# Conv sequence, frequency gate: product and sum on GpSimd, ScalarE in emission order, inverse roots by logarithm and exponential

## The chip, the core and the metric

The kernel runs on one core of one Trainium2 chip. Such a core has five engines with queues of their own: TensorE (PE, matrix products; its weight loads are shown apart as PEld), VectorE (DVE), ScalarE (ACT), GpSimd (POOL) and SyncE (SP, which here issues most DMAs). The metric is the device time of one execution in microseconds; lower is better. Times of several runs are given as a median with the lowest and the highest.

## The reference, cut to what matters

Four layers follow each other on `x` of shape 4 x 192 x 64 x 64 (image, channel, row, column). Layer 0 is a deformable convolution with an attention over channels and an MLP; layer 1 a non-local block over all 4096 pixels; layer 2 a window attention, a frequency gate and a gated MLP; layer 3 a small convolution whose weights come from the image's mean. The change lies in the frequency gate of layer 2 and what stands around it:

```python
def _hft(x, w, b):
    a = 3.0 * x
    for s in (2, 4, 8):
        pool = x.reshape(B, C, h // s, s, ww // s, s).mean(axis=(3, 5))
        a = a - jnp.repeat(jnp.repeat(pool, s, axis=2), s, axis=3)
    return jax.nn.sigmoid(_dwconv3(a, w, b)) * x

out = (o_img / s_img[:, :, None]).reshape(B, C, H, W)
out = _hft(_conv1x1(out, proj_w, proj_b), hft_w, hft_b)
x1 = x + out
z = jax.nn.gelu(_conv1x1(_ln_c(x1, n2g, n2b), fc1_w, fc1_b), approximate=False)
```

So the attention's output is projected (a 1x1 convolution), three pooled versions of it are taken off three times itself, a depthwise 3x3 convolution and a sigmoid make a gate of that, the gate multiplies the projection, and the product is added to the image. A layer norm over the channels and the MLP follow. A layer norm needs `1 / sqrt(variance + 1e-5)` at each pixel.

## The kernel before

The four images go through the layers one after the other. While image `b` is in its last part, `rest` (projection with the gate, MLP, layer 3), parts of image `b + 1` are woven in: `rest` pulls steps of two generators, `main` (image `b`) and `other` (`mlp0`, the layer-0 MLP of image `b + 1`), and takes a step of `other` whenever the numbers yielded by `main` add up to 1. The last image has nothing beside it (`alone`), and there a part of the depthwise taps is done on PE as products with diagonal matrices (`HFT_PE`, L1368) instead of DVE.

`project` works on six units. Units 0 to 3 are sixteen rows each of channels 0 to 127; units 4 and 5 hold the remaining 64 channels, two halves of the image on the two halves of the partitions. Every unit is 128 partitions x 1024 numbers. For each unit there are two steps:

- `first(u)`: two projected halves on PE (L1475, L1478), copied out of PSUM by ACT with the bias into `pr` (L1482); the pooling sums by DVE (L1490, L1493) and their way back (L1499); three times `pr` by ACT (L1505) and minus the means by DVE (L1513) into `hft`, or into `others` in the image's tile `x` for units 4 and 5; then `share(u)` copies rows at the units' edges, by GpSimd (L1454, L1455) or, for units 4 and 5, by DMAs that SP issues (L1466).
- `second(u)`: the depthwise convolution `depthwise_steps` by DVE into `acc` (named `ha` in the profile; L1373 the first tap, L1377 the others), the sigmoid by ACT (L1523), the product with `pr` (L1525) and the sum into `x` (L1526), both by DVE.

They are emitted in this order: first 0, first 1, second 0, first 2, second 1, first 4, first 5, second 4, first 3, second 2, second 5, then `ahead` (the layer norm of the first pair of rows for the MLP, `pair_norm_steps`, tiles `d_l2n` and `r_l2n`), second 3. `pr` has four buffers, `acc` two.

In which order the instructions of an engine stand in its queue is decided when the program is built: a scheduler chooses by its own estimates of costs, unless code stands inside `tc.manual_schedule()`, where an engine keeps the order of emission. The window attention before `project` and the MLP after it are inside such blocks, for all engines; `project` is not. Whatever the order, each queue is worked off in order.

ScalarE evaluates functions from a table set, and a change of the set is an instruction of its own (ACT_TABLE_LOAD in the profile). The list `in_order` tells whether a part is emitted in order. If it isn't empty, `table(name)` emits a load whenever the set changes, and `inverse_root_steps` takes logarithm and exponential on ACT (L353, L354, one table set for both). If it is empty, `table` does nothing, the loads are put in by the compiler, and the inverse root is a square root on ACT (L362) and a reciprocal on DVE (L364):

```python
if in_order:
    inverse_root(r, pv)
    yield VARIANCE
else:
    nc.scalar.activation(r, pv, AF.Sqrt, bias=eps)
    yield VARIANCE
    nc.vector.reciprocal(r, r)
```

The layer norms that `mlp0` computes while `project` runs (`norm_steps`, tiles `xa`, `d_l0m`, `r_l0m`; L793, L796) use the same function. Other names of `mlp0` in the profile: `h` (L844, L851) and `gl` (L858) are the widened activations before and after GELU, `o` the narrowed output or the attention's, which L874, L775 and L786 add into `xa`; L894 stores `xa`.

Of the kernel before, what the change touches and what calls it, by code (L numbers as in the profile page):

```python
# [12 lines left out]
AF = mybir.ActivationFunctionType  # L13
ALU = mybir.AluOpType
# [16 lines left out]
UN = UR * W  # L31
HEADS = 6
NEG = -1.0e30
LN_EXP, GELU = "natural_log_exp_and_others", "gelu"

# [40 lines left out]
GATE_PE, GATE_PE_LAST, HFT_PE = (0, 1), (0, 1, 2, 3, 4), (0, 1, 2, 3, 4)  # L78
# [3 lines left out]
def conv_seq_kernel(ctx: ExitStack, tc: tile.TileContext, a, out: bass.AP):  # L82
    nc = tc.nc

    def pool_of(**kw):

        return tc.tile_pool(**({} if kw.get("space") == DRAM else {"reuse_waits": "tile"}), **kw)
# [251 lines left out]
    in_order = []  # L339

    def table(name):

        if in_order and in_order[0] != name:
            in_order[0] = name
            if name == GELU:
                nc.scalar.preload_act_table(AF.Gelu)
            else:
                nc.scalar.preload_act_table_set(name)

    def inverse_root(r, pv):  # L350

        table(LN_EXP)
        nc.scalar.activation(r, pv, AF.Ln, bias=eps)  # L353
        nc.scalar.activation(r, r, AF.Exp, scale=-0.5)  # L354
# [64 lines left out]
    def links(steps, upto=None):  # L419

        while True:
            try:
                link = next(steps)
                if upto is not None and link == upto:
                    return None
            except StopIteration as end:
                return end.value
# [311 lines left out]
    def mlp0(b, m2, pool, sb, ps):  # L739
# [95 lines left out]
        for i in range(NCH):  # L835
# [3 lines left out]
            def widen(ms):  # L839

                banks = [ps.tile([128, 2, HN], F32, tag="h", name=f"h_{b}_{i}_{ms[0]}_{q}") for q in range(2)]
                for j, m in enumerate(ms):
                    for q in range(2):
                        nc.tensor.matmul(  # L844
                            banks[q][:, j, :], lhsT=fc1[:, 0, bass.ts(m, 128)], rhs=hn[:, bass.ts(q, HN)], start=j == 0,
                            stop=False, skip_group_check=True,
                        )
                for j, m in enumerate(ms):
                    for q in range(2):
                        rows = slice(Q * q, Q * q + Q)  # L850
                        nc.tensor.matmul(  # L851
                            banks[q][:, j, :], lhsT=fc1[rows, 1, bass.ts(m, 128)], rhs=hn[rows, CN:], start=False, stop=True,
                            skip_group_check=True,
                        )
                for j, m in enumerate(ms):
                    for q in range(2):
                        table(GELU)
                        nc.scalar.activation(  # L858
                            gl[:, m, bass.ts(q, HN)], banks[q][:, j, :], AF.Gelu, bias=fc1_bias[:, m : m + 1]
                        )  # L860
# [189 lines left out]
    def windows(b, oi, load_image):  # L1050
# [3 lines left out]
        with ExitStack() as s:  # L1054
# [227 lines left out]
            with tc.manual_schedule():  # L1282
# [3 lines left out]
                norm(0, SQUARE)  # L1286
                in_order.append(None)
                table(LN_EXP)
                norm(0, VARIANCE)
                keep_warm(warm, 2)  # L1290
# [60 lines left out]
    def depthwise_steps(strip, w, diag, taps, acc, ps, name):  # L1351


        parts, blocks, rows = strip.shape[0], strip.shape[1], strip.shape[2] - 2
        acc = acc.rearrange("p (b r c) -> p b r c", b=blocks, c=W)

        def src(tap, b=slice(None), r=0, n=rows):
            return strip[:, b, tap // 3 + r : tap // 3 + r + n, tap % 3 : tap % 3 + W]

        others = [tap for tap in range(9) if tap not in taps]  # L1360
        first = others.pop(0)
        if taps:
            n = CN // W
            for b in range(blocks):
                for r in range(0, rows, n):
                    p = ps.tile([128, CN], F32, tag="t", name=f"{name}_{b}_{r}")[:parts]
                    for j, tap in enumerate(taps):
                        nc.tensor.matmul(p, lhsT=diag[:, j, :], rhs=src(tap, b, r, n), start=j == 0, stop=j == len(taps) - 1)  # L1368
                    to, p = acc[:, b, r : r + n], p.rearrange("p (r c) -> p r c", c=W)
                    nc.vector.scalar_tensor_tensor(to, src(first, b, r, n), w[:, first : first + 1], p, ALU.mult, ALU.add)  # L1370
        else:
            for b in range(blocks):
                nc.vector.tensor_scalar_mul(acc[:, b], src(first, b), w[:, first : first + 1])  # L1373
        yield first
        for tap in others:
            for b in range(blocks):
                nc.vector.scalar_tensor_tensor(acc[:, b], src(tap, b), w[:, tap : tap + 1], acc[:, b], ALU.mult, ALU.add)  # L1377
            yield tap
# [44 lines left out]
    def project(b, x, others, oi, ps, taps, ahead):  # L1423
# [3 lines left out]
        with ExitStack() as s:  # L1427
# [5 lines left out]
            tiles, prs = {}, {}  # L1433
            row = slice(1, W + 1)

            def get(u):

                if u not in tiles:
                    t = tiles[u] = held[:, u % 3] if u < 4 else others[:, u - 4]
                    nc.gpsimd.memset(t[:, :, :, 0:1], 0.0)  # L1440
                    nc.gpsimd.memset(t[:, :, :, W + 1 : W + 2], 0.0)

                    for v, parts, k, r in (
                        (0, slice(0, M), 0, 0), (3, slice(0, M), 0, UR + 1), (4, half(0), 0, 0), (5, half(1), 1, 9),
                    ):
                        if u == v:
                            nc.gpsimd.memset(t[parts, k, r, row], 0.0)
                return tiles[u]
# [67 lines left out]
            def second(u):  # L1516
                k = u // 4
                acc = sb.tile([M, UN], F32, tag="acc", name=f"ha_{b}_{u}")
                diag = hft_diag[:, k] if taps else None
                for tap in depthwise_steps(get(u), VW["l2_hftw"][:, k], diag, taps, acc, ps, f"ht_{b}_{u}"):  # L1520
                    if tap % 3 == 2:
                        yield
                nc.scalar.activation(acc, acc, AF.Sigmoid, bias=VW["l2_hftb"][:, k])  # L1523
                cols = bass.ts(u, UN)
                nc.vector.tensor_tensor(acc, acc, prs.pop(u), ALU.mult)  # L1525
                nc.vector.tensor_tensor(x[:, cols], x[:, cols], acc, ALU.add)  # L1526


            for of, u in (
                (first, 0), (first, 1), (second, 0), (first, 2), (second, 1), (first, 4), (first, 5), (second, 4),  # L1530
                (first, 3), (second, 2), (second, 5), (None, 0), (second, 3),
            ):
                if of is first:
                    first(u)
                    yield 0.33
                elif of is second:
                    for _ in second(u):
                        yield 0.5
                else:
                    ahead()  # L1540
# [306 lines left out]
    def rest(b, x, others, oi, sums, m2):  # L1847


        with ExitStack() as s:  # L1850
            alone = m2 is None
            sb = s.enter_context(pool_of(name="norms", bufs=1))
            ps = s.enter_context(pool_of(name="restps", bufs=2, space=PSUM))
            wide = s.enter_context(pool_of(name="restps2", bufs=5, space=PSUM))
            psums = Psums({"n": ps, "v": ps, "h": wide}, {"t": "h"})
            other = iter(())
            if not alone:
                other = mlp0(b + 1, m2, s.enter_context(pool_of(name="l0d", bufs=1)), sb, psums)
            credit = 0.0

            def main():
                hn = []

                def ahead():
                    hn.append(links(pair_norm_steps(x, 0, sb, psums, f"l2n2_{b}_0")))

                yield from project(b, x, others, oi.pop(), psums, HFT_PE if alone else (), ahead)
                yield from mlp(b, x, sums, sb, psums, GATE_PE if alone else (), hn)
                yield from layer3(b, x, sums, psums, alone)

            for part in main():
                credit += part
                while credit >= 1.0:
                    next(other, None)
                    credit -= 1.0
            for _ in other:
                pass
# [53 lines left out]
    for b in range(B):  # L1931
# [25 lines left out]
        x = big.tile([M, UNITS * UN + 2 * 2 * 10 * (W + 2)], F32, tag="x", name=f"x_{b}")  # L1957
        others = x[:, UNITS * UN :].rearrange("p (v k r c) -> p v k r c", v=2, k=2, c=W + 2)
# [9 lines left out]
        oi = big.tile([P, 2, HW], F32, tag="x", name=f"oi_{b}")  # L1968
# [79 lines left out]
```

## Time and profile before

| | |
|---|---|
| median of 3 runs | 6800.64 us (6798.39 to 6806.05) |
| the profiled execution | 6757.88 us, span from first to last instruction 6756.1 us |
| busy share of the span | PE 91%, PEld 62%, DVE 69%, ACT 53%, POOL 31% |
| mean granted PE clock | 0.952 |
| chain that ended last, by engine | PE 51%, DVE 17%, ACT 4%, issue 4%, DMA 2% |
| `project` runs, from the first L1475 on | 1866, 3460, 5044 and 6339 us after the start, for 105 to 134 us each |
| sigmoids L1523 | 24 x, median 1149 ns |
| products L1525 | 24 x, median 1218 ns |

A profile is of one execution. Its page gives the busy time of each engine, the chain of work that ended last (followed back from the last instruction, at each step to what released it), and groups of instructions with their number, busy time, mean duration, and the idle time of the engine just before them with what ended it. The same can be asked for a stretch of time. Engines work beside each other: only what lies on the chain of a stretch sets its end.

### The profile page before, as it was taken

Reading aid. Unit: us, or ns where it says so; the run is one execution under the profiler, and the core shown is the slowest. Engines: PE = TensorE matmul, PEld = TensorE weight load, DVE = VectorE, ACT = ScalarE, POOL = GpSimd, SP = SyncE. Lnnn points to the kernel's source line nnn. Section 1 sums busy time; section 2 is a strip of 40 time slices with the busy share of each in tenths; the row PEclk is TensorE's granted clock in tenths of the full one; section 3 lists DMA queues with packets and bytes.
Section 4 is the critical chain, followed back from the end, with each engine's and each line's share of the span. In section 5 each row is a group of like instructions: output and inputs, shape, how many; then the busy total and the mean of one; then the engine's idle time right before and its main releaser. Section 6 shows DMA issues by size and latency. Waiting matters only on the chain.

```text
span 6756.1 us, 115795 instructions
## 1 busy us (share of the span) xinstructions
PE 6155.1 (91%) x45392; PEld 4180.0 (62%) x45392; DVE 4694.1 (69%) x6908; ACT 3599.2 (53%) x6136; POOL 2065.4 (31%) x2276
## 2 busy tenths in 40 slices
PE   7687999999989899999998899999998889999986
PEld 4455578786644458887654457878664457776532
DVE  3664279985677758996576848988567867765656
ACT  3664368774444358885444338877444435544332
POOL 2654057662200027672210007765220000012200
PEclk8788999999989899999999999999999999999998
DMA  6885156661010156663110047665101010010000
GB/s 188 260 280 177 54 177 217 215 196 42 8 43 15 59 181 200 219 211 93 29 31 26 17 132 218 216 208 165 35 24 30 17 54 10 15 28 22 4 7 21
DMA packets 330496, 699.37 MB, mean 104 GB/s; under 512 B 60077, under 2 KB 217181, under 8 KB 329182
## 3 DMA queue, kind: packets, MB, share of 16 engines
q0 software_dynamic: 92736, 455.22, 21.0%
q1 hardware_dynamic: 236382, 235.95, 12.3%
q8 instruction: 358, 5.87, 0.4%
q14 instruction: 188, 1.54, 0.1%
q10 hardware_dynamic: 832, 0.79, 0.0%
HBM read 611.25 MB, written 78.87 MB: 102 GB/s over the span
## 4 chain that ended last, share of the span: by engine, by line
PE 51%; DVE 17%; ACT 4%; issue 4%; DMA 2%; SPq 0%; POOL 0%; another core or an unknown queue 0%; DVEq 0%; ACTq 0%; POOLq 0%
PE y L1031 8%; PE s L963 7%; PE h L634 3%; PE v L1196 2%; PE h L1574 2%; DVE ha L1377 2%; PE qk L1121 2%; PE qk L1122 2%; PE t L1204 1%; DVE gate L1377 1%; PE zm L1586 1%; DVE ga L1377 1%; PE h L1576 1%; PE s L1157 1%; PE rb L1270 1%
## 5 line engine op out<-in xcount | busy, mean ns | idle before, releaser
L616 POOL DMA_INDIRECT ring<-table,idx x1152 | 1634.7, 1419 | 1132.5 <-issue 217.8
L963 PE MATMUL s<-ths,ph 96*128 96x256 f32 x4096 | 991.5, 383 | 8.5 <-ACT xo L626 2.7
L963 PEld LDWEIGHTS s<-ths,ph 96*128 96x128 f32 x4096 | 784.0, 193 | 137.1 <-ACT ths L957 4.7
L622 ACT ACTIVATE row<-ring,pos 128x384 f32<-128x384 f32 x1152 | 672.0, 608 | 204.3 <-DVE xo L627 111.3
L1031 PE MATMUL y<-sc,gx 128*97 128x256 f32 x3008 | 724.7, 383 | 18.4 <-ACT yn L1037 15.1
L623 DVE SCALAR_TENSOR_TENSOR row<-ring,fr,row 128x384 f32<-128x384 f32 x1152 | 674.8, 613 | 91.6 <-ACT row L622 63.1
L1031 PEld LDWEIGHTS y<-sc,gx 128*97 128x97 f32 x3008 | 492.5, 165 | 150.8 <-ACT yn L1037 16.5
L626 ACT ACTIVATE xo<-row,pos 128x192 f32<-128x192 f32 x1152 | 485.8, 448 | 156.9 <-remote 63.8
L627 DVE SCALAR_TENSOR_TENSOR xo<-row,fr,xo 128x192 f32<-128x192 f32 x1152 | 447.1, 412 | 123.3 <-issue 60.6
L1028 DVE TENSOR_TENSOR sc<-sc,mbs 128x1024 f32<-128x1024 f32 x376 | 453.4, 1218 | 46.1 <-ACT mbs L989 26.5
L965 ACT COPY sc<-s 128x1024 f32<-128x1024 f32 x376 | 377.5, 1004 | 177.5 <-PE s L963 141.5
L970 DVE TENSOR_TENSOR top<-top,sc 128x1024 f32<-128x1024 f32 x282 | 344.5, 1222 | 137.4 <-ACT sc L965 115.9
L634 PE MATMUL h<-ti,xo 128*128 128x192 f32 x2304 | 437.1, 328 | 0.0
L1029 ACT ACTIVATE sc<-sc 128x1024 f32<-128x1024 f32 x376 | 393.4, 1053 | 75.6 <-DVE sc L1028 66.5
L634 PEld LDWEIGHTS h<-ti,xo 128*128 128x128 f32 x2304 | 390.9, 190 | 29.0 <-issue 8.6
L1180 DVE TENSOR_REDUCE es<-ex 128x6 f32<-128x384 f32 x264 | 133.3, 546 | 365.0 <-ACT ex L1176 365.0
L634 PE MATMUL h<-kept,xo 128*128 128x192 f32 x960 | 255.9, 402 | 114.1 <-DVE xo L627 61.5
L634 PEld LDWEIGHTS h<-kept,xo 128*128 128x128 f32 x960 | 183.0, 224 | 209.5 <-DVE xo L627 98.6
L1624 POOL COPY gate<-gate 128x192 f32<-128x192 f32 x12 | 4.2, 351 | 1000.4 <-ACT gate L1617 855.0
L1377 DVE SCALAR_TENSOR_TENSOR ga<-gate,v,ga 128x1024 f32<-128x1024 f32 x234 | 300.4, 1284 | 6.7
L1031 PE MATMUL y<-se,gx 128*97 128x256 f32 x1088 | 268.3, 387 | 8.6 <-ACT se L1029 8.1
L858 ACT ACTIVATE gl<-h,bias_fc 128x256 f32<-128x256 f32 x384 | 151.2, 474 | 232.9 <-PE h L851 232.5
(391 smaller groups left out, 11213.0 us busy)
## 6 DMA issues: line engine op xcount, KB each, us to landing
ti<-table SPq DMA_DIRECT2D x768, 48.0 KB
ring<-table,idx POOLq DMA_INDIRECT x1152
xnd<-xn SPq DMA_DIRECT2D x4, 3270.0 KB
xi<-in_x_dram SPq DMA_DIRECT2D x32, 384.0 KB
xk<-xd SPq DMA_DIRECT2D x32, 384.0 KB
xd<-xc SPq DMA_DIRECT2D x64, 192.0 KB
table<-tt SPq DMA_DIRECT2D x32, 384.0 KB
xc<-xd SPq DMA_DIRECT2D x60, 192.0 KB
```

Of the source, the lines that this page charges most:

```text
L616: nc.gpsimd.indirect_dma_start(out=gt.rearrange("p q r c -> p (q r c)"), out_offset=None, in_=corners, in_offset=bass.IndirectOffsetOnAxis ...
L622: nc.scalar.activation(row, gt[:, 0], AF.Copy, scale=pos[:, t, 9 + tap : 10 + tap])
L623: nc.vector.scalar_tensor_tensor(row, gt[:, 1], fr[:, t, 9 + tap : 10 + tap], row, ALU.mult, ALU.add)
L626: nc.scalar.activation(xo[:, j, :], row[:, 0, :], AF.Copy, scale=pos[:, t, tap : tap + 1])
L627: nc.vector.scalar_tensor_tensor(xo[:, j, :], row[:, 1, :], fr[:, t, tap : tap + 1], xo[:, j, :], ALU.mult, ALU.add)
L634: nc.tensor.matmul(acc[m // 2][:, bass.ts(m % 2, C)], lhsT=xo.rearrange("p j c -> p (j c)")[:, bass.ts(m, 128)], rhs=tt, start=t == 0 and ...
L963: nc.tensor.matmul(p[:, t, :], lhsT=ph[:, bass.ts(G * g + t, 128)], rhs=ths[i], start=True, stop=True)
L965: nc.scalar.copy(to, p)
L1028: nc.vector.tensor_tensor(ex, ex, mbs[i].unsqueeze(1).to_broadcast([128, G, QN]), ALU.add)
L1029: nc.scalar.activation(ex, ex, AF.Exp)
L1031: nc.tensor.matmul(py, lhsT=gx[:, G * g + t, :], rhs=ex[:, t, :], start=g == 0 and t == 0, stop=g == NG - 1 and t == G - 1,)
L1377: nc.vector.scalar_tensor_tensor(acc[:, b], src(tap, b), w[:, tap : tap + 1], acc[:, b], ALU.mult, ALU.add)
```

## The change

The product and the sum at the end of `second` go from VectorE to GpSimd. In `project`, ScalarE keeps the order of emission, with whatever of `mlp0` is emitted meanwhile; the other engines' order is still the scheduler's. `in_order` is not empty there any more: so table loads are emitted by `table` (the sigmoid has got its own name for that), and inverse roots in this part, those of `mlp0` included, are by logarithm and exponential.

```diff
-LN_EXP, GELU = "natural_log_exp_and_others", "gelu"
+LN_EXP, GELU, SIGMOID = "natural_log_exp_and_others", AF.Gelu, AF.Sigmoid
...
-            if name == GELU:
-                nc.scalar.preload_act_table(AF.Gelu)
+            if name in (GELU, SIGMOID):
+                nc.scalar.preload_act_table(name)
             else:
                 nc.scalar.preload_act_table_set(name)
...
+                table(SIGMOID)
                 nc.scalar.activation(acc, acc, AF.Sigmoid, bias=VW["l2_hftb"][:, k])
                 cols = bass.ts(u, UN)
-                nc.vector.tensor_tensor(acc, acc, prs.pop(u), ALU.mult)
-                nc.vector.tensor_tensor(x[:, cols], x[:, cols], acc, ALU.add)
+                nc.gpsimd.tensor_mul(acc, acc, prs.pop(u))
+                nc.gpsimd.tensor_add(x[:, cols], x[:, cols], acc)
...
-                yield from project(b, x, others, oi.pop(), psums, HFT_PE if alone else (), ahead)
+                with tc.manual_schedule(engines={mybir.EngineType.Activation}):
+                    in_order.append(None)
+                    yield from project(b, x, others, oi.pop(), psums, HFT_PE if alone else (), ahead)
+                    in_order.pop()
                 yield from mlp(b, x, sums, sb, psums, GATE_PE if alone else (), hn)
```

## The prediction

> **What bounds the kernel now.** I read the page first, then the busy time of the engines in the four stretches in which the projection (`project`) runs, then the groups of instructions inside them, then the chain of waits at their ends, and last the timeline where GpSimd and VectorE touch SBUF together. The page gives PE 91% of the span and the chain 51% PE, 17% DVE; but the change touches only the four projection stretches, together 474 of 6756 us. Busy times there (columns: stretch, its us, PE, weight loads, DVE, ACT, POOL, granted clock, DMA share, GB/s):
>
> ```profile
> 1866.00:1992.00 126.00, 103.44 (x425) 55.45 (x424) 117.57 (x198) 54.73 (x73) 4.40 (x12) 0.87 0.17 45
> 3460.00:3583.00 123.00, 97.29 (x419) 52.36 (x418) 116.56 (x196) 54.73 (x73) 4.40 (x12) 0.89 0.16 45
> 5044.00:5169.00 125.00, 102.51 (x421) 54.51 (x419) 116.31 (x195) 54.74 (x73) 4.39 (x12) 0.87 0.15 42
> 6337.00:6437.00 100.00, 87.13 (x217) 37.07 (x218) 70.56 (x128) 25.76 (x28) 11.75 (x29) 0.90 0.06 15
> ```
>
> In the first three (images 0 to 2, woven with the next image's MLP) DVE is busy 117 of 125 us and sets the pace; 6.5 us of its idle time is the wait for the first projected tile. In the last (image 3, alone, part of the taps on PE) no engine is full: DVE and PE take turns. ACT is half idle, POOL nearly empty. What DVE does in the first stretch, and ACT:
>
> ```profile
> L1377 DVE SCALAR_TENSOR_TENSOR ha<-hft,wide,ha 128x1024 f32<-128x1024 f32 x30 | 38.2, 1274 | 0.4
> L1525 DVE TENSOR_TENSOR ha<-ha,pr 128x1024 f32<-128x1024 f32 x5 | 6.1, 1217 | 0.0
> L1526 DVE TENSOR_TENSOR x<-x,ha 128x1024 f32<-128x1024 f32 x5 | 6.0, 1207 | 0.0
> L364 DVE RECIPROCAL r_l0m<-r_l0m 128x128 f32<-128x128 f32 x3 | 2.8, 947 | 0.0
> L364 DVE RECIPROCAL r_l2n<-r_l2n 128x256 f32<-128x256 f32 x1 | 1.8, 1753 | 0.9 <-ACT r_l2n L362 0.9
> ```
>
> ```profile
> L858 ACT ACTIVATE gl<-h,bias_fc 128x256 f32<-128x256 f32 x28 | 11.2, 475 | 15.3 <-PE h L851 15.2
> L1482 ACT ACTIVATE pr<-pp,wide 128x512 f32<-128x512 f32 x12 | 8.2, 686 | 11.8 <-PE pp L1475 11.0 <-PE pp L1478 0.8
> L1523 ACT ACT_TABLE_LOAD x5 | 6.4, 1283 | 0.1
> ```
>
> Products, sums and reciprocals stand between the taps without a gap: what leaves DVE there leaves the path. The end of the stretch, in the chain of waits (start, us, what):
>
> ```profile
> 1997.14 1.16 ACT ha L1523
> 1998.32 1.24 DVE ha L1525
> 1999.63 1.28 ACT L1580
> ```
>
> Sigmoid, product, then the table load of the MLP's first GELU: the last unit's product is on the path, its sum is not.
>
> **What leaves DVE.** A woven stage has six units. Five products and five sums lie among the taps: 5 x 1.217 + 5 x 1.207 = 12.1 us; the sixth product is counted at the end of the stage. Reciprocals: 3 x 0.947 + 1.753 = 4.6 us. The idle times before r_l2n's reciprocal (0.9) and before a `pr` (0.5) go too. Together 18.1 us a stage.
>
> **What GpSimd takes.** The trace has two sizes of the same operation on GpSimd (min/median/max ns):
>
> ```profile
> L161 POOL TENSOR_TENSOR pixels<-pixels,ident x2: 312/314/315, 4.3 to 5.5; 128x64 f32<-128x64 f32 x2
> L1244 POOL TENSOR_TENSOR ot<-ot,ot x80: 446/456/1172, 1656.5 to 6332.0; 102x128 f32<-102x128 f32 x40, 96x128 f32<-96x128 f32 x40
> ```
>
> 64 elements 314 ns, 128 elements 449: 2.11 ns an element. For 1024 that gives 449 + 896 x 2.11 = 2.34 us. With the slope of GpSimd's copies (16 elements 198 ns, 528 elements 640: 0.86) it would be 1.22; I take 2.34, the same operation, and keep 1.22 for the range. Twelve of them are 28 us of a 126 us stage, so POOL has the time. The question is what they do to DVE. L1171 on DVE (two SBUF inputs) takes 957 ns alone; beside GpSimd's adds:
>
> ```profile
> 1829.24 1.58 POOL L1244 TENSOR_TENSOR ot<-ot,ot 102x128 f32<-102x128 f32 x2 [14.01 <-ACT ot L1238]
> 1829.49 1.02 DVE L1171 TENSOR_TENSOR ex<-ex,mx 128x768 f32<-128x768 f32 x1
> ...
> 1849.87 1.58 POOL L1244 TENSOR_TENSOR ot<-ot,ot 102x128 f32<-102x128 f32 x2 [12.32 <-ACT ot L1238]
> 1850.07 1.08 DVE L1171 TENSOR_TENSOR ex<-ex,mx 128x768 f32<-128x768 f32 x1
> ```
>
> The first add (454 ns) ends 205 ns after DVE's start in the upper pair, 263 in the lower; DVE is 63 and 122 ns longer. So DVE stands still until some 142 ns before the add's end. The second add, normally 450 ns, ends 310 ns after DVE's end: it too stood still, but for 140 ns. They take turns. With 2.34 us an operation, each costs a back-to-back DVE 2.34 - 0.14 - 0.14 = 2.06 us, against the 1.21 that it saves. DVE operations with one input in PSUM do not take part (L398 runs at 1216 ns around GpSimd work, 1217 alone).
>
> The Trainium skill (SBUF — State Buffer, section "SBUF: two separate sides") says that the pair of ports that VectorE and GpSimd share is an exclusive lock, held for the whole instruction, and that the loser blocks fully. By that the price would be the whole 2.34 us, some 0.3 more an operation and 2.4 more a stage; the rows show DVE resuming before the end.
>
> Where they fall, by the order in which the changed kernel, as built, queues its instructions on each engine: units 0, 4 and 2 are followed by taps and pooling sums, all with two SBUF inputs: 2 x 2.06 each, 12.4. After unit 1 DVE waits anyway (next paragraph), which hides most of the product: 0.75 + 2.06 = 2.8. After unit 5 come 3.6 us of DVE work on PSUM, which hides one of two: 2.06. Unit 3 is the end. Sum 17.2 us a stage.
>
> **ScalarE's order.** In emission order unit 4's `pr` (L1482) stands behind unit 1's sigmoid, which waits for unit 1's last tap, and DVE's next instruction after that tap is the pooling of that `pr`: sigmoid 1.15 + 2 x 0.686 + hops 0.1 = 2.6 us of new wait. Before, `pr` ran ahead of the sigmoid. For units 2 and 3 DVE has 7 and 3 us of taps in between: nothing; without that cover 2.6 each. Unit 4's first taps now follow its halo exchange (L1466, five issues by SP) after 1.2 us of other DVE work; before, the second of them began 3.4 us after the last L1513. I put 1.3 us there; 0 to 2.2 is possible. SP's stores of `xa` change places with these issues, covered by the twelve taps of 0.67 us.
>
> Table loads in a woven stage go from 15 to 18, and four exponentials (0.31 to 0.42 us) are added: 5.2 us on an engine with 71 us idle. A load runs while ACT waits (0.1 us idle before five of them), so nothing is added; if each stood in front of a `pr`, 3.9.
>
> The Trainium skill (ScalarE: Activation LUTs, "What ACT_TABLE_LOAD costs") puts a drain of about 1.38 us on top of each load. By that the three extra loads would be 8 us of ACT time, still inside its idle time; no such gap stands at the loads here.
>
> **End of a stage.** The last product on GpSimd instead of DVE: 2.34 - 1.24 = 1.1 us, nothing hides it. POOL's queue holds the gate's memsets (which wait for the last L1475) ahead of unit 4's product, and the halo copies L1454/L1455 behind a sum, which ends some 3 us before the copies' tile is ready; so nothing. If the sum is late, its 2.3 us fall on the next taps.
>
> **Sum.** Woven stage: -18.1 + 17.2 + 2.6 + 1.3 + 1.1 = +4.1; three of them +12.3. Image 3: from unit 0's last tap (6366.05) to PE's taps of unit 4 (6388.54) DVE is the chain, with two products and two sums, 4.9 us. In their place stand, for units 0 and 1, the wait for `pr` behind the sigmoid (2.6), 0.85 more until the product lets go, and a sum (2.06): 11.0. So +6.1; later PE's taps are the bound and cover the rest, and at the end -1.67 (reciprocal) + 0.42 + 1.1 cancel. Total +18.4 us. The profiled execution took 6757.88 us (span 6756.1), 0.6% under the median of 6800.64; the difference is added to the median: 6819.
>
> **Rivals.** (a) *Side by side*: a long GpSimd operation does not hold DVE as the short ones did. Then the stage is -18.1 + 5.0 = -13.1, image 3 about 0, in all -39: 6761. For it: DVE is 93% busy in three stages. Against: L1171 above. It turns at a hold of about 1.45 us an operation, where the sum is nil. (b) *Part of the hold is hidden*: 20 of DVE's 117 us read PSUM; if most of them fall under GpSimd's work, 7 us a stage go, and the total is near -3: 6798, no difference. This is also the outcome if the order moves little. (c) *ScalarE blocks*: ACT waits 15.2 us a stage for PE in front of GELUs; in emission order a group of those stands ahead of nearly every sigmoid, and of `pr` of units 2 and 5. If half reaches DVE, +7.6 a stage, +23 over the sum: 6842.
>
> **Chances.** The forecast 0.47, (a) 0.18, (b) 0.22, (c) 0.13. A measurement here tells about 0.2%, 13.6 us, from no change. So faster 0.18, same 0.22, slower 0.60. The likeliest case alone holds 6806 to 6832 (hold 1.9 to 2.2 us, halo 0 to 2.2). The range goes down into (a), where a hold of 1.22 us less its overlaps leads, and up past (c): 6773 to 6850.
>
> **What would show it.** Right: L1377 `ha` and L1490 longer than 1274 and 686 ns on average (by some 17 us a stage in sum), GpSimd's products near 2.3 us when alone and 3 to 3.6 when they wait, DVE idle for ACT `pr` L1482 up by 2 to 3 us, POOL 28 us a stage, the four stretches longer by 4, 4, 4 and 6 us. Wrong: L1377 at 1.28 us beside GpSimd's products, or stretches shorter by 10 us or more.

## The result, and the profile after

The changed kernel takes 6854.48 us (median of six runs, 6807.52 to 6870.63); the runs of the kernel before beside it have a median of 6803.35. The ratio is 1.0072, with a 95% interval of 1.0045 to 1.0100: slower by 51 us, between 31 and 68. The direction was forecast, the size was not: 18 us were, and the time lies above the range's upper end of 6850. One run of a later kernel (the roots only) took 9987 us at a granted clock of 0.561; ratios leave it out.

The two profiled executions (6757.88 and 6807.52 us, the fastest of the six) differ by 49.6 us, but 21 us of that stand ahead of the first changed instruction (the expectation of the null run below says 13; that run shows that such differences come without any change). So the stages are compared, not the spans. For each projection stretch I took many instructions that both kernels execute, ahead of it and behind it, and asked by how much more the second kernel is late behind it than ahead of it. The four stretches grew by 8.8, 8.0, 7.6 and 11.7 us, 36 in all; in the last, the figure moves by 1 us or so with the instructions that are taken. The same stretches after, between the same instructions (stretch, its us, PE, weight loads, DVE, ACT, POOL, granted clock, DMA share, GB/s):

```profile
1887.00:2021.80 134.80, 109.85 (x439) 57.47 (x439) 119.93 (x186) 59.28 (x80) 35.05 (x22) 0.88 0.15 42
3483.80:3614.80 131.00, 107.02 (x433) 55.82 (x433) 119.36 (x186) 59.16 (x80) 34.17 (x22) 0.91 0.15 42
5079.40:5211.90 132.50, 106.93 (x430) 56.06 (x430) 118.71 (x184) 59.27 (x80) 35.04 (x22) 0.89 0.14 39
6374.80:6485.30 110.50, 88.76 (x221) 37.35 (x222) 71.59 (x118) 25.62 (x29) 35.07 (x39) 0.88 0.05 14
```

DVE has a dozen instructions less than in the stretches of before and is busy no less: what it lost in work it spends standing still inside its instructions. POOL went from 4.4 to 35 us. Groups of DVE in the first stretch of before (the one of the taps on `hft` stands in the prediction), then of after (line, operation, count, busy us, mean ns, idle time ahead of them):

```profile
L1377 DVE SCALAR_TENSOR_TENSOR ha<-x,wide,ha 128x512 f32<-128x512 f32 x32 | 21.7, 744 | 0.0
L1490 DVE TENSOR_TENSOR pt<-pr 128x512 f32<-128x512 f32 x6 | 4.1, 686 | 5.3 <-ACT pr L1482 5.3
L1493 DVE TENSOR_TENSOR pq<-pt 128x256 f32<-128x256 f32 x6 | 2.5, 421 | 0.0
```

```profile
L1377 DVE SCALAR_TENSOR_TENSOR ha<-hft,wide,ha 128x1024 f32<-128x1024 f32 x30 | 42.4, 1412 | 0.7
L1377 DVE SCALAR_TENSOR_TENSOR ha<-x,wide,ha 128x512 f32<-128x512 f32 x32 | 25.4, 854 | 0.0
L1490 DVE TENSOR_TENSOR pt<-pr 128x512 f32<-128x512 f32 x6 | 9.5, 1591 | 6.5 <-ACT pr L1482 6.5
L1493 DVE TENSOR_TENSOR pq<-pt 128x256 f32<-128x256 f32 x6 | 4.6, 759 | 0.1
```

The same taps and pooling sums, which took 38.2 + 21.7 + 4.1 + 2.5 us, take 4.2 + 3.7 + 5.4 + 2.1 = 15.4 us more. GpSimd's side, and one pair in the timeline (start, us):

```profile
L1526 POOL TENSOR_TENSOR ha<-ha,pr 128x1024 f32<-128x1024 f32 x5 | 16.1, 3222 | 25.2 <-ACT ha L1524 25.2
L1527 POOL TENSOR_TENSOR x<-x,ha 128x1024 f32<-128x1024 f32 x5 | 14.5, 2898 | 0.4
```

```profile
1921.67 2.72 POOL L1526 TENSOR_TENSOR ha<-ha,pr 128x1024 f32<-128x1024 f32 x1 [4.58 <-ACT ha L1524]
1924.47 3.23 POOL L1527 TENSOR_TENSOR x<-x,ha 128x1024 f32<-128x1024 f32 x1
1925.40 2.85 DVE L1490 TENSOR_TENSOR pt<-pr 128x512 f32<-128x512 f32 x1
```

Alone, a product takes 2.34 us (the last one of each stretch), as estimated from the two short ones. Beside DVE both engines stretch. L1490, normally 0.69 us, begins at 1925.40 under the sum, which ends at 1927.70, and ends at 1928.25, so it resumed at about 1927.56, 0.14 us before the sum's end. That is the pattern of the short operations in the trace of before.

### The profile page after: what moved, and what is told of

Read it like the earlier page. It is cut to its first block, busy times and chain, and to the rows that moved or that the text cites. A ratio compares the mean times of both kernels' runs of the same rounds, so it can differ in the third digit from the quotient of the medians.

```text
span 6805.6 us, 115883 instructions
## 1 busy us (share of the span) xinstructions
PE 6163.1 (91%) x45392; PEld 4184.2 (61%) x45392; DVE 4687.0 (69%) x6847; ACT 3610.8 (53%) x6158; POOL 2181.2 (32%) x2324
```

## The experiments

Behind the first comparison stand three groups of runs, each on one chip with its own runs of the kernel before; ratios are against those. "Stretches" are the differences of the four projection stretches to the profile of before, taken as above.

| kernel | ratio to before (95%) | stretches, us | sum |
|---|---|---|---|
| changed, first time | 1.0072 (1.0045 to 1.0100) | +8.8 +8.0 +7.6 +11.7 | +36.1 |
| before, as a null | 0.9987 (0.9967 to 1.0007) | +1.0 +2.1 -1.4 -0.2 | +1.5 |
| product and sum on GpSimd only | 1.0090 (1.0068 to 1.0112) | +11.2 +13.1 +9.8 +9.6 | +43.7 |
| ScalarE's order and roots only | 1.0027 (1.0007 to 1.0048) | +3.4 +4.1 +1.7 0.0 | +9.2 |
| roots only | 1.0006 (0.9985 to 1.0027) | -3.4 -0.8 -4.3 -4.0 | -12.5 |
| roots only, again | 1.0015 (0.9994 to 1.0036) | -4.9 -1.9 -4.3 -2.4 | -13.5 |
| changed, product back on DVE | 1.0097 (1.0072 to 1.0122) | +5.7 +8.8 +4.1 +7.2 | +25.8 |
| changed, again | 1.0080 (1.0052 to 1.0108) | +8.7 +11.3 +4.5 +12.0 | +36.5 |
| before, 16 filling matmuls | 0.9991 (0.9978 to 1.0003) | -2.4 +3.4 -1.6 -2.3 | -2.9 |
| changed, 16 filling matmuls | 1.0026 (1.0007 to 1.0045) | +9.0 +11.1 +8.9 +8.4 | +37.4 |
| roots only, 16 filling matmuls | 0.9970 (0.9954 to 0.9986) | -4.0 -3.0 -6.7 -2.3 | -16.0 |

The scheduler builds the queues anew for each kernel. In the first stretch, only the kernels with filling matmuls or scratch work keep DVE's order of before when nothing else is changed; in the others some 25 to 40 of the 190 instructions stand elsewhere. So a difference between two of these kernels holds that too.

**The kernel before, as a null.** No edit.

> The kernel before, unchanged, run as if it were a changed one. The stages of the projection grew by 8.9, 8.0, 8.8 and about 12 us in the profile after, 38 us together, while the medians differ by 51 and the two profiles by 49.5, of which 13 us stand before the first changed instruction. Theory: the 12 to 13 us beyond the 38 are chance in the granted clock and in the gathers. Then this run stands within 0.2% of before, its single runs spread over 15 us or more, and its profile differs from that of before by some microseconds in stages without any change, with the projection stretches equal to within 0.5 us. Rival: the changed kernel draws the clock down (its timed runs had 0.944 to 0.948). Then all runs of this one show 0.950 or more and spread less than 10 us.

The median stands within the bound, and single runs go from 6774 to 6835 us with mean granted clocks of 0.945 to 0.953. Its profile is 62 us longer than that of before: stages without any change differ by up to 23 us, the longer ones with more half clock in them. The stretches differ by up to 2.1 us, not by 0.5, and by up to 3.4 in the kernel before with filling matmuls, whose edit lies outside of them: that is the error of every stretch in the table, and some 3 us that of a sum. So 13 or 20 us between two profiles are nothing, 8 in a stretch are something. The rival isn't refuted by this; the filling matmuls below come back to it.

**Product and sum on GpSimd only.**

```diff
-                nc.vector.tensor_tensor(acc, acc, prs.pop(u), ALU.mult)
-                nc.vector.tensor_tensor(x[:, cols], x[:, cols], acc, ALU.add)
+                nc.gpsimd.tensor_mul(acc, acc, prs.pop(u))
+                nc.gpsimd.tensor_add(x[:, cols], x[:, cols], acc)
```

> Only the product and the sum go to GpSimd; ScalarE stays in the scheduler's order, the roots stay Sqrt and reciprocal. Theory (the turns between GpSimd and VectorE are the main cost): a woven stretch loses 11.3 us of VectorE work (ten instructions at 1.13 net of overlap) and gains 16.6 us of longer VectorE instructions, 2.2 us of wait for the sum ahead of the next norm and 1.2 at the end: +7 to +9 each, image 3 +3 to +8, total +24 to +35 us. Rival (the waits behind ScalarE's order are the main cost): the stretches change by -2 to +2, total within 10 us of before.

The rival falls: with ScalarE in the scheduler's order the stretches grow by 9.6 to 13.1 us, more than with the whole change. DVE's instructions became longer there too: in image 0 it loses 11.3 us of work and is nevertheless busy 6.8 us more.

**ScalarE's order and roots only; roots only.** The first is the changed kernel with the two lines above put back on DVE. The second is the kernel before with this:

```diff
+    in_project = []
...
-        if in_order:
+        if in_order or in_project:
             inverse_root(r, pv)
...
+                in_project.append(None)
                 yield from project(...)
+                in_project.pop()
```

> Only ScalarE's emission order and the roots by Ln and Exp; product and sum stay on VectorE. Theory (turns are the main cost): a woven stretch loses 4.3 us of reciprocals and 0.2 us of idle time, and gains 2.4 us of wait for pr behind a sigmoid and 2.2 us of wait for the halo exchange: -1 to +1 each; image 3 waits three times for pr, 2.4 us each, of which the product on VectorE covers about half: +2 to +5; total -1 to +8 us. Rival (ScalarE's order is the main cost): +5 or more in each stretch, total +20 or more.

> Only the roots by Ln and Exp, ScalarE in the scheduler's order, product and sum on VectorE. Theory: VectorE loses 4.3 us of reciprocals in each woven stretch and 0.2 us of idle time, image 3 loses about 1 us: stretches -4 to -5, -4 to -5, -4 to -5 and -1 to 0, total -12 to -16 us, 0.2% faster than before. Rival: the additional table loads (1.28 us each) land in front of sigmoids or pr on the path, up to four a stretch: -4.5 + 5.1, total within 4 us of before or slower.

The roots alone do in the stretches what was expected: 12.5 us less. With ScalarE in emission order the same roots end at +9.2, so the order, with the queues that come with it, costs about 22 us. Of the waits that make it, the one for the next norm of `mlp0` was not in my list (waits of DVE in the first stretch of the kernel with order and roots: who, for what, us, times, longest):

```profile
DVE d_l0m L793 <- PE pb_l0m L382: 2.8, 1, 2.8
DVE ha L1526 <- ACT ha L1524: 2.4, 2, 1.2
DVE d_l2n L1419 <- PE pb_l2n L1418: 0.8, 2, 0.4
```

But both kernels are slower in their medians than their stretches say, by 14 and some 20 us. Both profiles have 61 us of half clock where the next stage of image 3 begins, and so has the one with GpSimd only. TensorE's wait in front of that stage and the windows behind it, in the kernel with the roots only and then in that of before:

```profile
5554.27 3.32 PE L912 MATMUL tp<-xk,phiT 96*96 96x512 f32 x4 [2.88 <-DMA xk<-xd]
```

```profile
5554.00:5616.00 62.00, 61.17 (x177) 41.43 (x178) 4.46 (x8) 6.95 (x10) 0.00 (x0) 0.51 0.20 59
5616.00:5640.00 24.00, 23.91 (x114) 20.53 (x113) 17.28 (x18) 15.33 (x18) 0.00 (x0) 1.00 0.00 1
```

```profile
5514.35 1.96 PE L910 MATMUL tp<-xk,phiT 96*96 96x512 f32 x4 [1.46 <-DMA xk<-xd]
```

```profile
5514.00:5545.00 31.00, 30.09 (x169) 21.14 (x170) 4.46 (x8) 5.94 (x9) 0.00 (x0) 1.00 0.44 121
```

The same four products take 3.32 instead of 1.96 us, and the granted clock is 0.51 for 62 us.

**Work beside DVE that nobody reads.** The kernel before, with two GpSimd operations behind each unit of image 0 and 1 that write a scratch tile. It ran once, for its profile, so it has no ratio.

```diff
+            scratch = s1.tile([M, UN], F32, tag="scratch", name=f"scratch_{b}")
...
-                nc.vector.tensor_tensor(acc, acc, prs.pop(u), ALU.mult)
+                pr = prs.pop(u)
+                nc.vector.tensor_tensor(acc, acc, pr, ALU.mult)
...
+                if b == 0:
+                    for _ in range(2):
+                        nc.gpsimd.tensor_mul(scratch, pr, pr)
+                if b == 1:
+                    for _ in range(2):
+                        nc.gpsimd.tensor_copy(scratch, pr)
```

> The kernel before with extra GpSimd work whose result nobody reads, put behind each of the six units of a projection stretch: in image 0 twelve two-input products of 128x1024, in image 1 twelve one-input copies of 128x1024, in images 2 and 3 nothing. Theory (GpSimd and VectorE take turns, the whole instruction long, where both have two SBUF inputs): image 0's stretch grows by 12 to 24 us (11 such operations made VectorE 16.6 us longer in the changed kernel), all of it as longer VectorE instructions; image 1's by 0 to 6, since the halo copies (0.6 us) never made a VectorE instruction beside them longer. Image 2's stays within 1 us. Rival (VectorE is late in the changed kernel because it waits for results, the GpSimd work itself costs it nothing): image 0's stretch stays within 2 us.

Image 0's stretch grew by 19.7 us, 18.9 of it as longer DVE instructions (1.58 us for each of the twelve), image 2's by -2.4. Nobody waits for these results, and DVE's queue has the order of before, so the rival falls: the GpSimd operation itself holds DVE up. The part on copies was wrong: image 1's stretch grew by 9.6 us, 8.7 of it inside DVE's instructions, 0.73 for each copy of about 1.05 us. One input is enough on either side; here the first tap L1373, which has one tensor input and takes 0.74 us alone, beside the second of two products:

```profile
1898.21 7.38 POOL L1531 TENSOR_TENSOR scratch<-pr 128x1024 f32<-128x1024 f32 x2
```

```profile
1903.76 2.38 DVE L1373 TENSOR_SCALAR ha<-hft,wide 128x1024 f32<-128x1024 f32 x1
```

**The changed kernel with the product on DVE.**

```diff
-                nc.gpsimd.tensor_mul(acc, acc, prs.pop(u))
+                nc.vector.tensor_tensor(acc, acc, prs.pop(u), ALU.mult)
```

> The changed kernel with the product on VectorE again: only the sum is on GpSimd. Theory (each GpSimd operation costs VectorE some 1.5 to 2 us and saves it 1.13): between ScalarE's order alone (+3.4, +4.1, +1.7, 0 us in the four stretches) and the changed kernel (+8.8, +8.0, +7.6, +11): about +6, +6, +5 and +5, 22 us in all. Rival (the cost is the chain sigmoid, product, sum through GpSimd, whose product comes late): the stretches are as with ScalarE's order alone, within 1.5 us each.

+25.8 us, between the two as the theory had it (22). The sum alone costs 17 us on top of ScalarE's order, the product 10 more. Its profile has 58 us of half clock at the entry of image 3's next stage. Its median is 69 us above before: more than its stretches and that half clock (28 us in its profile) make, and the rest stays open.

**The changed kernel, and the one with the roots only, again.** No edit; another chip.

> The changed kernel once more, unchanged, for more timed runs beside the kernel before and a second profile. Theory (the four stretches cost 36 us, the rest of the 51 is chance in the clock): stretches +8 to +9 three times and +10 to +12 again, the median 30 to 45 us above before. Rival (a clock drawn down by the change adds to it): 50 us or more above before, mean granted clock of its runs lower than before's by 0.002 or more.

> The kernel with only the roots by Ln and Exp once more. Its first profile had stretches shorter by 3.4, 0.8, 4.3 and 4.0 us, but also 61 us of half clock at the entry of image 3's next stage, which before lacks, and its median was no lower than before's. Theory (that episode is chance): the stretches are shorter by 12 to 14 us again, and the median is 5 to 20 us below before. Rival (the change brings the episode on): the episode is there again, and the median is not below before.

The stretches come back, to within 1 us in the sums and 3.3 us in each. The medians again lie above them: 56 against 36, and 17 against -13. The episode of 61 us is there again in the roots' profile and not in that of the changed kernel. So in both cases what was named as the rival came: the changed kernel is more than 50 us slower, at a median granted clock of 0.956 against 0.960, and the roots bring the episode on. So far, then, in image 3: five profiles with TensorE idle for 2.5 to 2.9 us in front of that stage, all five with 58 to 61 us of half clock behind it; five with 1.5 to 2.4 us, with 0 or 7. In images 1 and 2 it is 1.6 to 2.4 us, with 0 to 17.

**Filling that idle time.** `mlp0` already ends with matmuls that only fill it; four more in the kernel before, in the changed one, and in the one with the roots only.

```diff
-                keep_warm(p[:, 0:384], 12)
+                keep_warm(p[:, 0:384], 16)
```

> The kernel before with 16 instead of 12 filling matmuls at the end of mlp0 (L896), where TensorE waits for the DMA of the next stage's first tile. Each is 0.67 us, so 2.7 us more. In the profiles so far TensorE is idle there for 1.5 to 2.9 us in images 1 to 3, and where the idle time was 2.5 us or more the clock stood at half for 58 to 61 us behind it (five profiles of five, 26 us lost each time), in the others for 0, 7 or 17 us. Theory (the idle time brings the half clock on): the idle time is 0 to 0.3 us, no half clock of 17 us or more follows it, and the kernel is 5 to 16 us below before (two episodes of 17 us less, some 8 us each, and 2.7 us lost in image 0, which has no idle time there). Rival (the half clock comes from the load of the dense stage): the episodes stay, the kernel is 3 to 8 us slower.

> The changed kernel with the same 16 filling matmuls. Theory (the four stretches cost 36 us and the rest of the measured difference is half clock at the entries): stretches +8 to +9, +8 to +11, +5 to +9, +11 to +12 us against the profile of before, and the median 30 to 40 us above that of the kernel before with 16 filling matmuls. Rival (the change costs more than its stretches show): 45 us or more above it.

> The kernel with only the roots by Ln and Exp, and the 16 filling matmuls: the version that should beat both. Theory: the stretches are 12 to 14 us shorter, the 61 us of half clock at the entry of image 3's next stage are gone, and the median is 10 to 18 us below the kernel before with 16 filling matmuls, 20 to 30 us (0.3 to 0.45%) below before. Rival (the table switches cost something outside the stretches): not below the kernel before with 16 filling matmuls.

In all three profiles TensorE goes from the filling matmuls to the stage without idle time in images 1 to 3, and no half clock follows there. Image 3 of the kernel before with 16 (start, us, what):

```profile
5507.71 1.78 PE L737 MATMUL o<-bias,ident 128*128 128x384 f32 x5
5509.33 1.88 PE L910 MATMUL tp<-xk,phiT 96*96 96x512 f32 x4
```

Medians: 6747.07 for the kernel before with 16 (6755.06 without), 6783.57 for the changed one, 6739.22 for the roots. With the entries alike, the change costs 6783.57 - 6747.07 = 36.5 us (some 20 to 45 by the scatter of these runs): what its stretches show (37). The roots with the filling are 15.8 us faster than before, 0.9970 (0.9954 to 0.9986): the one version that beats both kernels. The filling alone gave 8 us, inside the 5 to 16 expected but not clear of no change; the roots on top of it gave 8 instead of 10 to 18. In image 0 the idle time lies out of the filling's reach, 8 us behind the entry: 2.1 to 2.8 us in front of L915 in the three profiles, with 51 us of half clock behind it; before has 1.6 there and none. Of the ten profiles without the filling three have 27 to 48 us of half clock there and seven none, one of these with 2.3 us of idle time. Whether the filling has a part in the 51 us wasn't tried.

## Why the forecast had the direction and too little of the size

The step that failed is the sum of DVE's waits, together with what leaves DVE. In a woven stage the forecast had 3.9 us of new waits (2.6 for `pr`, 1.3 for the halo exchange), nothing for the norm, and 18.1 us that leave DVE; in image 0 the new waits are 7.5 us, and 16.5 us leave. In image 3 it took the rest of the stage as covered by TensorE's taps; DVE's waits there grew by 10.0 us.

Three parts of the sum can be set against runs (us over all four stretches; the first column adds the terms of the forecast by part, both idle times of 0.9 and 0.5 us with the reciprocals, and without its rounding in image 3):

| part | forecast | measured | from |
|---|---|---|---|
| reciprocals off DVE | -19.3 | -13 | roots only, twice |
| ScalarE's order | +16.9 | +22 | order and roots, less roots |
| product and sum on GpSimd | +20.6 | +27 | change, less order and roots |
| sum | +18.2 | +36 | |

**The hold on DVE was right.** The forecast had 17.2 us a woven stage. In image 0 the DVE instructions of after are 16.6 us longer, and the scratch work shows that this is the price of the GpSimd operation and not of a wait. An operation that DVE meets back to back costs it 1.98 to 2.17 us, forecast 2.06; only the 2.06 for unit 5 became 0.2 and, as below, a wait. Rival (a), side by side, and (b), half hidden, are refuted by the stretches of every kernel with GpSimd in it. The rule of the Trainium skill (SBUF — State Buffer, section "SBUF: two separate sides") that the loser blocks for the whole instruction agrees to within the 0.14 us above. It also says that who starts first has the lock. The trace adds that GpSimd can lose for long. Unit 2's product was queued behind taps that follow each other without a gap:

```profile
1990.14 6.19 POOL L1526 TENSOR_TENSOR ha<-ha,pr 128x1024 f32<-128x1024 f32 x1 [6.09 <-ACT ha L1524]
```

```profile
1988.73 5.39 DVE L1377 SCALAR_TENSOR_TENSOR ha<-x,wide,ha 128x512 f32<-128x512 f32 x8
1994.27 0.48 DVE L874 SCALAR_TENSOR_TENSOR xa<-o,wide,xa 128x256 f32<-128x256 f32 x1
```

It ends at 1996.33, 2.34 us after 1993.99: it waited 3.85 us, until the run of taps had ended and, 0.15 us later, L874 came, which reads PSUM. The same product waits 3.8 us in images 1 and 2 too. These taps overlap by 0.08 us each, but that alone isn't the reason: in the kernel with only the sum on GpSimd, the sum came in between two such taps after 0.45 us. What decides it stays open.

**The gain was too high.** DVE's instructions overlap by 0.08 us where they follow each other, so products, sums and reciprocals took 15.6 us of its time in image 0, not the 16.7 that their durations add up to. The idle time of 0.85 us in front of the last reciprocal went, but came back as a wait: the same norm is waited for one step later (L1419, 0.7).

**The waits were the larger miss in the woven stages.** DVE's waits in the first stretch of after:

```profile
DVE pt L1490 <- ACT pr L1482: 6.5, 2, 4.2
DVE oi L1273 <- PE rb L1270: 2.3, 2, 1.4
DVE d_l2n L1399 <- PE pm_l2n L1395: 2.2, 1, 2.2
DVE ha L1373 <- DMA x<-x: 2.2, 1, 2.2
DVE d_l2n L1419 <- PE pb_l2n L1418: 0.7, 1, 0.7
```

Of the first, 4.2 us stand in before too (the first tile); the other, 2.4, is the `pr` behind a sigmoid, forecast at 2.6. The halo exchange was put at 1.3 and took 2.2, the end of its range. The norm's wait for a sum that GpSimd finishes late (2.2) was not in the sum: I had let DVE's PSUM work hide one of unit 5's two operations and counted 2.06 for the other; instead the wait for the result took its place. In images 1 and 2 the new waits for `pr` are 3.3 and 2.4 us, for the halo exchange 2.2 and 2.1, for the norm 0 and 2.3.

Added up for image 0, from the first pooling sum to the last tap: -15.6 of instructions, +16.6 of longer ones, +7.5 of new waits, -1.6 of old ones, +0.7 of short gaps: 7.5 us. The end of the stage adds 1.4.

**The end of the stage was right by luck.** The forecast's 1.1 us is the longer product. From the start of the last sigmoid to the first `z` it takes 3.60 us after, and took 3.78 before: the MLP's table load stood behind the product (1999.63 in the prediction's chain) and is now emitted ahead of the wait for it, so it runs beside it.

```profile
2025.66 1.15 ACT L1524 ACTIVATE ha<-ha,wide 128x1024 f32<-128x1024 f32 x1 [6.41 <-DVE ha L1377]
2026.83 1.28 ACT L1581 ACT_TABLE_LOAD   x1
2029.26 2.42 ACT L1581 ACTIVATE z<-h,bias_fc1T 128x512 f32<-128x512 f32 x4 [1.15 <-POOL ha L1526]
```

What is lost there is lost on TensorE. It waits longer for `z`, and the six products behind the wait take 2.93 us instead of 1.56, with a granted clock of 0.61 from 2030 to 2034; before, then after:

```profile
2001.66 1.56 PE L844 MATMUL h<-d_l0m,fc 128*128 128x256 f32 x6 [0.75 <-ACT z L1580]
```

```profile
2030.00 2.93 PE L844 MATMUL h<-d_l0m,fc 128*128 128x256 f32 x6 [4.59 <-ACT z L1581]
```

In images 1 and 2 it is the same 2.93 and 4.59 us.

**Image 3 was wrong by its cover.** I took 6.1 us up to unit 4's first PE taps, and "later PE's taps are the bound and cover the rest". Up to there it is 6.7 us. The rest was not covered. The waits of DVE in image 3's stretch, before and after:

```profile
DVE ha L1370 <- PE ht L1368: 15.2, 6, 6.4
DVE pt L1490 <- ACT pr L1482: 9.3, 1, 9.3
DVE d_l2n L1419 <- PE pb_l2n L1418: 1.3, 2, 1.1
DVE ha L1525 <- ACT ha L1523: 1.2, 1, 1.2
```

```profile
DVE pt L1490 <- ACT pr L1482: 15.6, 4, 8.4
DVE ha L1370 <- PE ht L1368: 13.2, 4, 6.4
DVE d_l2n L1419 <- PE pb_l2n L1418: 7.3, 1, 7.3
```

A third `pr` stands behind a sigmoid (three new waits of 2.4), and DVE, which before filled the norm's time with a product, a sum, a reciprocal and taps, now waits 7.3 us for it. DVE's wait for PE's taps shrank only by 2. Without the first tile's wait (9.3 and 8.4): +7.2 +6.0 -2.0 -1.2 = +10.0 us.

**The span is not the sum of its stretches.** The remaining 15 us of the 51 (20 of 56 in the second comparison) are not in the stretches, and with TensorE's idle time in front of the next stage filled 36.5 us are left. For the changed kernel this is not clear of noise: 36 lies within the 31 to 68 of its own comparison. For the roots it is: 7 and 17 us above before without the filling, 8 below with it. The forecast added nothing for stages that the change doesn't touch. That the half clock behind such entries takes part is shown by the filling; why the idle time is longer in some kernels, and which entries made the 15 us in the timed runs of the changed kernel (its two profiles have at most 17 us of half clock at an entry), stays open.

**Rival (c)**, ScalarE blocks, at 6842 was nearest to the measured time, but not by its mechanism: the order costs 22 us and not the 40 that its two parts (17 and 23) make, and the waits are for `pr`, the halo exchange and norms.

## What to carry to other kernels

By these runs, moving elementwise work from a full VectorE to an idle GpSimd pays only if the GpSimd operation, less some 0.3 us, is shorter than the VectorE operation that it replaces, wherever VectorE works on SBUF; here 2.34 us (a hold of about 2.06) stood against 1.21. A queue put into emission order is priced by going through each of its instructions and naming who waits behind it, norms and other generators' steps included, and "cover" is taken as nothing until the row that covers is named with its length. Changes of some 0.2% in a kernel whose clock wanders are judged by stretches between the same instructions, and the stage behind a changed stretch is looked at for its clock.

## What the hardware showed that I had not expected

- The granted clock stays at half for 58 to 61 us with TensorE busy 61.17 of 62 us, and the four products at the start take 3.32 instead of 1.96 us. The Trainium skill (TensorE: Matmul & The Clock Gate, "What's actually happening") says that one busy window of about 3.4 us releases the clock; by that figure some 18 such windows passed here (an estimate: 61 by 3.4). The products there are 96x96, not 128x128; whether that is the reason wasn't tried.
- An idle time of 2.5 to 2.9 us in front of a dense stage was followed by that in five profiles of five (all in image 3), one of 1.5 to 2.4 us by 0 to 17 us of half clock; without idle time the clock stayed full there (images 1 to 3). In image 0 the idle time doesn't decide alone: 2.1 us, 8 us behind the entry, were followed by 51 us of half clock, 2.3 us in another kernel by none.
- A GpSimd copy with one input holds VectorE too (0.73 us for each of 1.05), and a VectorE operation with one SBUF tensor is held (2.38 us instead of 0.74).
- GpSimd can wait through several VectorE instructions that start after it: 3.85 us behind taps, until their run had ended. In other places it came in after one.
